# Lines of 65 words instead of 64 for two sources of weights, and an image loaded in chunks

## The chip, the cores and the metric

The kernel runs on one core of one Trainium2 chip. Times are device microseconds (us) of one execution. Before the change the median of three runs was 7750.35 us (7748.62 to 7756.67). Experiments ran in three jobs, each with its own runs of the kernel before on the same chip.

TensorE is called PE where it multiplies and PEld where it loads weights; DVE is VectorE, ACT ScalarE, POOL GpSimd, SP SyncE.

## The reference, cut to what matters

Eight images of 128 x 128 tokens with 64 channels pass two layers in fp32. The first is an attention along columns and rows, which the change does not touch. The second is this:

```python
h = _pw(_ln(x, g1, b1), w_te, b_te)                      # norm over channels, 64 -> 128
F = jnp.fft.fft2(h.astype(jnp.complex64), axes=(1, 2))
fr = jnp.concatenate([jnp.real(F), jnp.imag(F)], axis=-1)
fc = gelu(_pw(fr, w_fc, b_fc))                           # a 256 x 256 map per frequency
sp = jnp.real(jnp.fft.ifft2(re + 1j * im, axes=(1, 2)))  # re, im: the halves of fc
x1 = x + _pw(sp, w_tp, b_tp)
h2 = _pw(_ln(x1, g2, b2), w_fe, b_fe)                    # the MLP: norm, 64 -> 128,
d = gelu(depthwise_conv_3x3(h2, w_dw) + b_dw)            # depthwise convolution,
return x1 + _pw(d, w_fp, b_fp)                           # 128 -> 64
```

## The kernel before

The transforms are products with cosine and sine tables. In both places of interest the data is the *stationary* operand: a channel of the normed image "xn", or of the spectrum "gt", is loaded into TensorE as weights, and the table streams past it. With the channel as the innermost axis, the 128 words of one channel lie 64 words apart.

```python
def load_norm(b):
    xn = xnp.tile([P, P, C], F32, tag="xn", name="xn")       # P = 128, C = 64, one buffer
    nc.sync.dma_start(out=xn, in_=x2[b])                     # 4 MB in one load
    images[b] = {"xn": xn}
    for h in range(0, P, CH):                                # CH = 8: 16 chunks
        norm(xn[:, h : h + CH, :], xn[:, h : h + CH, :], CH)
        yield
```

`norm(xo, xi, n)` reduces on DVE, subtracts the mean on POOL, squares on ACT, reduces again on DVE, and multiplies on POOL. The forward transform along h, in two halves of the frequencies, each followed by its frequency groups:

```python
gt = big.tile([P, 2, 64, C], F32, tag="gt", name="gt")
...
for c0 in range(0, C, 4):
    aps = ps_m.tile([P, 4, P], F32, tag="mm", name="aps")
    for c in range(4):
        nc.tensor.matmul(                                    # line 490
            aps[:, c, 0:nk], lhsT=xn[:, :, c0 + c], rhs=rw[:, first : first + nk],
            start=True, stop=True,
        )
    # evicted to "at" by DVE and ACT in turn
...
nc.scalar.copy(gt[:, :, k0 : k0 + n, :].rearrange("p t k c -> p k t c"), gps[:, 0:n, :, :])
```

The inverse transform:

```python
gr, gi = gt[:, 0, :, c0 + c], gt[:, 1, :, c0 + c]
both = gt.rearrange("p t k c -> p (t k) c")[:, :, c0 + c]
nc.tensor.matmul(yps[:, c, :], lhsT=both, rhs=cosn, start=True, stop=False)          # line 592
nc.tensor.matmul(yps[0:64, c, :], lhsT=gi, rhs=nsinn, start=False, stop=True)        # line 593
nc.tensor.matmul(yps[64:128, c, :], lhsT=gr, rhs=sinn, start=False, stop=True)       # line 594
```

The images follow one another. The MLP of one image and the norm of the image after it are admitted step by step beside the transforms:

```python
NORM_FROM = 20                       # the second step of the second half's groups
...
for i, _ in enumerate(fourier(b)):
    if i * (P // CH + 1) >= done * MLP_STEPS:
        next(before, None)           # the MLP of image b - 1
        done += 1
    if i >= NORM_FROM:
        next(after, None)            # the norm of image b + 1
```

A scheduler then orders the instructions of each engine, so an instruction may run well ahead of its place in this text if its data allow it.

Of the kernel before, what the change touches and what calls it, by code (L numbers as in the profile page):

```python
"""Criss-cross attention followed by a Fourier token mixer and a depthwise-convolution MLP.

Layer 0 attends, per token (h, w), over its image column (its own position excluded) and its row
with one softmax.  Both directions run through the same block routine with the attended axis on the
partitions; each keeps its own row maximum, and the two partial softmaxes are merged afterwards.

Layer 1 runs per image.  The channel maps of the spectral branch commute with the spatial
transforms, so w_te is applied behind the forward FFT (merged with w_fc) and w_tp in front of the
inverse one.  The input is real, so only the frequencies kw = 0..64 are transformed; the map at the
mirrored frequency -k sees the conjugate, i.e. the imaginary weights with the other sign, and the  # L10
real part of the inverse FFT needs only the Hermitian part (G(k) + conj G(-k)) / 2.
"""
# [10 lines left out]
F32 = mybir.dt.float32  # L23
# [4 lines left out]
PSUM = bass.MemoryType.PSUM  # L28
DRAM = bass.MemoryType.DRAM

P = 128
C = 64
D8 = 8
HID = 128
R = 32  # rows (or columns) of an attention block
NBLK = P // R
NEG = -1.0e30
EPS = 1e-3
# Frequencies along w, in the order they are stored in: 0 and 64 share a slot later.
KWS = [0, 64] + list(range(1, 64))  # L40
NKW = len(KWS)
CH = 8  # image rows of a chunk of the convolution
# Of the steps of one image's transforms: those that the MLP is spread over, and the first one behind
# the last use of the normed image.
MLP_STEPS = 28
# [3 lines left out]
def dft_tables():  # L49
    """cos/sin tables of the 128-point transforms; they depend on the shapes alone."""  # L50
    n = np.arange(P)
    kw = np.array(KWS)
    ang = 2.0 * np.pi * (np.outer(n, kw) % P) / P
    rw = np.stack([np.cos(ang), -np.sin(ang), -np.cos(ang)], axis=2).reshape(P, 3 * NKW)
    full = 2.0 * np.pi * (np.outer(n, n) % P) / P
    cos, sin = np.cos(full), np.sin(full)
    k = np.arange(64)
    back = 2.0 * np.pi * (np.outer(k, n) % P) / P
    re = 2.0 * np.cos(back) / P
    re[0] = 1.0 / P  # L60
    im = -2.0 * np.sin(back) / P
    im[0] = np.where(n % 2 == 0, 1.0, -1.0) / P
    idw = np.concatenate([re, im], axis=0)
    out = np.concatenate([rw, cos, sin, cos / P, sin / P, -sin / P, idw], axis=1)
    return np.ascontiguousarray(out.astype(np.float32))
# [5 lines left out]
def attention(tc, nc, x, w_q, b_q, w_k, b_k, w_v, b_v, gamma, x2):  # L71
    NB = x.shape[0]
    with ExitStack() as ctx:
        const = ctx.enter_context(tc.tile_pool(name="a_const", bufs=1))
        xpool = ctx.enter_context(tc.tile_pool(name="a_x", bufs=8))
        big = ctx.enter_context(tc.tile_pool(name="a_big", bufs=1))
        p2 = ctx.enter_context(tc.tile_pool(name="a_p2", bufs=2))
# [10 lines left out]

        # Rows 0-63 of a transposed pair hold the channels of one image line, rows 64-127 those of
        # the next one; the weights are block diagonal accordingly.  # L90
        wq = const.tile([P, 64], F32, tag="wq", name="wq")
# [10 lines left out]
        nc.gpsimd.memset(bq, 0.0)  # L102
        # Row 8 of every quadrant of the keys is a row of ones, which takes up the maximum.
        nc.gpsimd.memset(bk, 1.0)
# [27 lines left out]

        # Line r = 2 * (8 * (q // 2) + i) + q % 2 of a block lies in quadrant q at place i.
        def stage1(xb, mneg):
            """Queries, keys, values and the (negated) maxima of one block; yields between parts."""
            s = Block()
# [4 lines left out]
            for ic in range(2):  # L141
                for g in range(2):
                    jc = 2 * g + ic
                    tp = ps_m.tile([P, 4, P], F32, tag="mm", name="tp")
                    for jj in range(4):
                        r = 2 * (4 * jc + jj)
# [34 lines left out]
            for q in range(4):  # L181
                e = ps_e.tile([P, 8, P], F32, tag="e", name="e1")
                rows = slice(32 * q, 32 * q + D8)
# [16 lines left out]
            for q in range(4):  # L200
                nc.scalar.dma_start(
                    out=s.qt[32 * q + D8 : 32 * q + D8 + 1, :, :],
                    in_=mts[16 * (q // 2) + q % 2 : 16 * (q // 2) + 16 : 2, :],
# [3 lines left out]
        def stage2(s, y, masked):  # L207
            """Attention of one block, not yet divided by its sum (last column); yields between parts."""
            yv = y.rearrange("p (g i s) c -> p g s i c", g=2, s=2)
# [11 lines left out]
            for q in range(4):  # L221
                e = ps_e.tile([P, 8, P], F32, tag="e", name="e2")
                rows = slice(32 * q, 32 * q + D8 + 1)
                for a in range(2):
# [8 lines left out]
                    for j in range(4):  # L233
                        i = 4 * a + j
# [42 lines left out]
        def end(n):  # L277
            b, way, blk = tasks[n]
            s = state.pop(n)
# [16 lines left out]
            o.xs.append(s.xb)  # L296
            # Both partial sums are brought to the common maximum and divided by the common sum.
            cols = slice(blk * R, blk * R + R)
            mh, mw, dh, dw = o.mht[:, cols], s.mneg, o.dht[:, cols], y[:, :, C]
            t = p2.tile([P, 5, R], F32, tag="tsm", name="tsm")  # L300
# [37 lines left out]
        for n in range(len(tasks)):  # L338
            fetch(n + 3)
            parts = [end(n)]  # L340
# [6 lines left out]
def mixer(tc, nc, x2, tbl, prm, out):  # L347
# [3 lines left out]
    with ExitStack() as ctx:  # L351
# [29 lines left out]
        with tc.tile_pool(name="m_prep", bufs=1) as prep:  # L381
# [32 lines left out]

            # Biases of both norms go through the linear maps behind them.
            pv = ps_m.tile([P, 2], F32, tag="mm", name="pv")
# [8 lines left out]

            # w_te @ w_fc for the real and the imaginary half.
            nc.vector.tensor_scalar_mul(wte, wte, col[:, 0:1])
# [18 lines left out]
        def norm(xo, xi, n):  # L446
            """(xi - mean) / sqrt(var + eps) over the channels of n lines of tokens."""
            st = p2.tile([P, 3, CH], F32, tag="st", name="st", bufs=4)
            nc.vector.tensor_reduce(st[:, 0, 0:n], xi, AX.X, ALU.add)
            nc.vector.tensor_scalar_mul(st[:, 0, 0:n], st[:, 0, 0:n], 1.0 / C)  # L450
            nc.gpsimd.tensor_tensor(  # L451
                xo, xi, st[:, 0, 0:n].unsqueeze(2).to_broadcast([P, n, C]), ALU.subtract
            )
            sq = p2.tile([P, CH, C], F32, tag="sq", name="sq")
            nc.scalar.activation(sq[:, 0:n, :], xo, AF.Square)
            nc.vector.tensor_reduce(st[:, 1, 0:n], sq[:, 0:n, :], AX.X, ALU.add)
            nc.vector.tensor_scalar(st[:, 1, 0:n], st[:, 1, 0:n], 1.0 / C, EPS, ALU.mult, ALU.add)  # L457
            nc.gpsimd.tensor_tensor(st[:, 2, 0:n], st[:, 1, 0:n], mhalf[:, 0:n], ALU.pow)  # L458
            nc.gpsimd.tensor_tensor(  # L459
                xo, xo, st[:, 2, 0:n].unsqueeze(2).to_broadcast([P, n, C]), ALU.mult  # L460
            )
# [3 lines left out]
        def load_norm(b):  # L465
            xn = xnp.tile([P, P, C], F32, tag="xn", name="xn")
            nc.sync.dma_start(out=xn, in_=x2[b])
            images[b] = {"xn": xn}
            for h in range(0, P, CH):
                norm(xn[:, h : h + CH, :], xn[:, h : h + CH, :], CH)  # L470
                yield

        # Groups of frequencies that fill a PSUM bank, in two halves that share the buffer "at".
        groups = [KWS[0:2]] + [KWS[k : k + 4] for k in range(2, NKW, 4)]
        halves = [groups[:9], groups[9:]]

        def fourier(b):
            im = images[b]
            xn = im["xn"]
            gt = big.tile([P, 2, 64, C], F32, tag="gt", name="gt")  # L480
            for half_groups in halves:
# [20 lines left out]
                for g in half_groups + [None, None]:  # L502
# [45 lines left out]
                    if pend_tp is not None:  # L548
                        gg, (gr, gi) = pend_tp
                        gps = ps_m.tile([P, 4, 2, C], F32, tag="mm", name="gps")  # L550
                        if gg[0] == 0:
                            # kw = 0 and 64 have real inverse columns: they share one complex slot.
                            nc.tensor.matmul(gps[:, 0, 0, :], lhsT=gr[:, 0, 0:P], rhs=wtp, start=True, stop=False)
# [5 lines left out]
                        else:  # L559
# [7 lines left out]
                        nc.scalar.copy(  # L567
                            gt[:, :, k0 : k0 + n, :].rearrange("p t k c -> p k t c"), gps[:, 0:n, :, :]
                        )
# [39 lines left out]
        def lines(xs, lo, hi):  # L609
            """The rows lo..hi of an image held in two halves, as (offset, rows) pieces."""  # L610
            for s in range(2):
                a, z = max(lo, 64 * s), min(hi, 64 * s + 64)
                if a < z:
                    yield a - lo, xs[s][:, a - 64 * s : z - 64 * s, :]

        def mlp(b):
            """Chunks of image rows; the first half of a chunk goes ahead of the second half of the one before."""
            xs = images.pop(b)["x1"]

            def expand(k, prev):  # L620
# [9 lines left out]
                nc.scalar.copy(xt, tp)  # L630
                # Rows 8k-2 .. 8k+8 of the expanded image with a border of zeros.
                h2 = p2.tile([P, CH + 3, P + 2], F32, tag="h2", name="h2")
# [58 lines left out]

        # The MLP of an image runs beside the first part of the next image's transforms, and the norm
        # of the image after that beside the last part, when "xn" is free again.
        for _ in load_norm(0):
# [58 lines left out]
```

## Time and profile before

| | |
|---|---|
| median of three runs | 7750.35 us |
| attention, all images | until about 3850 us |
| first L490 (image 0) | 3941.3 us |
| one image of the mixer (its first L490 to that of the next image), mean of images 1 to 6 | 464.2 us |
| of it: first half of L490 (F1) / its groups | 54.5 / 138.3 us |
| second half of L490 (F2) / its groups | 54.1 / 129.7 us |
| inverse | 86.0 us |

The stage times come from the order of time: F1 and F2 last from the first to the end of the last L490 of a half, their groups from there to the next stage's first product, and the inverse from the first L592 to the end of the last L594. Some 1.75 us more pass before the next image's first L490. The prediction below shows the page's busy line, the windows of image 4 and the rows of the weight loads. A row of a line's loads gives shortest, median and longest duration in ns, then the first start and the last end in us. One more such row is needed later, that of the 64-column loads of the inverse:

```profile
L593 PEld LDWEIGHTS yps<-tb,gt x1024: 215/234/258, 4159.1 to 7463.3; 128*64 128x64 f32 x171
```

L490 is written 128 times an image, 1024 times in all, and counts x2048, two such records each.

### The profile page before, as it was taken

Reading aid. Unit: us, or ns where it says so; the run is one execution under the profiler, and the core shown is the slowest. Engines: PE = TensorE matmul, PEld = TensorE weight load, DVE = VectorE, ACT = ScalarE, POOL = GpSimd, SP = SyncE. Lnnn points to the kernel's source line nnn. Section 1 sums busy time; section 2 is a strip of 40 time slices with the busy share of each in tenths; the row PEclk is TensorE's granted clock in tenths of the full one; section 3 lists DMA queues with packets and bytes.
Section 4 is the critical chain, followed back from the end, with each engine's and each line's share of the span. In section 5 each row is a group of like instructions: output and inputs, shape, how many; then the busy total and the mean of one; then the engine's idle time right before and its main releaser. Section 6 shows DMA issues by size and latency. Waiting matters only on the chain. (4 is left out here: it accounts for less than half of the span.)

```text
span 7744.1 us, 73804 instructions
## 1 busy us (share of the span) xinstructions
PE 6559.2 (85%) x31019; PEld 5279.1 (68%) x31019; DVE 3369.5 (44%) x4376; ACT 1790.8 (23%) x2458; POOL 2176.4 (28%) x2050
## 2 busy tenths in 40 slices
PE   9999999999999999999668778787877878778774
PEld 7777878778787787777556566565665666566553
DVE  2232322323222232322222665756667565675757
ACT  1111111111111111111022433424333242433422
POOL 0020110201002020020244463544545345463423
PEclk6565555665556555555578778787887878778775
DMA  2010020100202001010100010100101010010000
GB/s 66 2 55 12 6 61 1 55 12 6 60 1 61 6 18 49 1 44 1 46 33 14 22 44 7 44 17 24 41 9 45 17 45 17 22 44 7 24 19 17
DMA packets 188189, 208.21 MB, mean 27 GB/s; under 512 B 141138, under 2 KB 176466, under 8 KB 176594
## 3 DMA queue, kind: packets, MB, share of 16 engines
q1 hardware_dynamic: 179154, 168.89, 7.6%
q0 software_dynamic: 4608, 33.56, 1.2%
q8 instruction: 244, 4.00, 0.2%
q10 hardware_dynamic: 4096, 1.06, 0.1%
q14 instruction: 87, 0.71, 0.0%
HBM read 135.32 MB, written 67.11 MB: 26 GB/s over the span
## 5 line engine op out<-in xcount | busy, mean ns | idle before, releaser
L666 DVE SCALAR_TENSOR_TENSOR acc<-h,wdw,acc 128x1024 f32<-128x1024 f32 (+2 forms) x1088 | 1502.5, 1404 | 33.6 <-ACT acc L664 23.1
L235 PEld LDWEIGHTS e<-qt,kt 9*128 9x128 f32 x4096 | 855.9, 315 | 248.3 <-issue 212.3
L235 PE MATMUL e<-qt,kt 9*128 9x128 f32 x4096 | 958.9, 422 | 70.0 <-DMA qt<-mts 45.5
L314 POOL TENSOR_TENSOR xb<-xb,yw 128x2048 f32<-128x2048 f32 x32 | 132.7, 4148 | 3009.5 <-issue 1918.9
L672 PE MATMUL op<-wfp,acc 128*128 128x64 f32 x2048 | 391.7, 371 | 672.8 <-ACT acc L669 672.8
L672 PEld LDWEIGHTS op<-wfp,acc 128*128 128x128 f32 x2048 | 378.9, 282 | 779.3 <-ACT acc L669 753.4
L218 PEld LDWEIGHTS yp<-v,att 128*128 128x128 f32 x4096 | 810.8, 303 | 132.0 <-ACT qt L177 90.5
L218 PE MATMUL yp<-v,att 128*128 128x65 f32 x4096 | 856.5, 393 | 0.0
L243 ACT ACTIVATE att<-e 128x1024 f32<-128x1024 f32 x256 | 261.9, 1023 | 1825.7 <-PE e L235 1825.7
L185 PEld LDWEIGHTS e<-kt,qt 8*128 8x128 f32 x4096 | 607.6, 256 | 69.9 <-issue 47.8
L185 PE MATMUL e<-kt,qt 8*128 8x128 f32 x4096 | 633.8, 353 | 14.9 <-DVE mh L188 14.9
L458 POOL TENSOR_TENSOR st<-st,mhalf 128x8 f32<-128x8 f32 x256 | 511.6, 1999 | 192.1 <-DVE st L457 128.4
L542 POOL TENSOR_TENSOR gl<-gl 128x512 f32<-128x512 f32 (+2 forms) x272 | 433.2, 1597 | 381.1 <-ACT gl L539 381.1
L490 PE MATMUL aps<-tb,xn 128*128 128x93 f32 (+1 forms) x2048 | 455.3, 405 | 80.1 <-POOL xn L459 80.1
L219 DVE COPY yh<-yp 128x260 f32<-128x260 f32 x256 | 109.6, 428 | 946.8 <-PE yp L218 946.8
L490 PEld LDWEIGHTS aps<-tb,xn 128*128 128x128 f32 x2048 | 453.3, 312 | 90.8 <-POOL xn L459 80.9
L676 POOL TENSOR_TENSOR ot<-x,bfp 128x512 f32<-128x512 f32 (+1 forms) x144 | 216.9, 1511 | 871.8 <-DVE x L607 609.3
L157 PE MATMUL vps<-wv,xt 128*128 128x130 f32 x2048 | 415.8, 373 | 43.3 <-DVE xt L151 43.3
L219 DVE COPY yw<-yp 128x260 f32<-128x260 f32 x256 | 109.6, 428 | 777.3 <-PE yp L218 777.3
L157 PEld LDWEIGHTS vps<-wv,xt 128*128 128x128 f32 x2048 | 372.9, 275 | 75.3 <-DVE xt L151 67.7
L607 DVE TENSOR_TENSOR x<-dps,x 128x256 f32<-128x256 f32 x256 | 167.5, 708 | 515.2 <-PE dps L601 515.2
L327 POOL TENSOR_TENSOR xb<-xb,tm 128x128 f32<-128x128 f32 x512 | 270.0, 580 | 409.9 <-DVE tm L322 409.9
(146 smaller groups left out, 9748.8 us busy)
## 6 DMA issues: line engine op xcount, KB each, us to landing
xb<-in_x_dram SPq DMA_DIRECT2D x32, 1024.0 KB
x<-xb POOLq DMA_DIRECT2D x32, 1024.0 KB, 7.3
x<-x SPq DMA_DIRECT2D x16, 2048.0 KB
xn<-x SPq DMA_DIRECT2D x8, 4096.0 KB
out_dram<-ot SPq DMA_DIRECT2D x120, 256.0 KB
qt<-mts ACTq DMA_DIRECT2D x256, 4.0 KB
out_dram<-ot SPq DMA_DIRECT2D x8, 224.0 KB
xb<-in_x_dram SPq DMA_DIRECT2D x32, 0.2 KB
```

The costliest lines, as they stand in the source:

```text
L157: nc.tensor.matmul(vps[:, jj // 2, o : o + 130], lhsT=xt[:, jj, :], rhs=wv2, start=True, stop=True)
L185: nc.tensor.matmul(e[:, i, :], lhsT=s.qt[rows, i, :], rhs=s.kt[rows, i, :], start=True, stop=True)
L218: nc.tensor.matmul(yp[:, j, :], lhsT=att[:, i, :], rhs=s.v[:, r, :], start=True, stop=True)
L219: nc.vector.tensor_copy(yv[:, q // 2, q % 2, 4 * a : 4 * a + 4, :], yp)
L235: nc.tensor.matmul(e[:, i, :], lhsT=s.kt[rows, i, :], rhs=s.qt[rows, i, :], start=not masked, stop=j == 3 or not masked,)
L243: nc.scalar.activation(att, e, AF.Exp)
L327: nc.gpsimd.tensor_tensor(xv, xv, tm[:, :, k * R : k * R + R], ALU.add)
L458: nc.gpsimd.tensor_tensor(st[:, 2, 0:n], st[:, 1, 0:n], mhalf[:, 0:n], ALU.pow)
L490: nc.tensor.matmul(aps[:, c, 0:nk], lhsT=xn[:, :, c0 + c], rhs=rw[:, first : first + nk], start=True, stop=True,)
L542: nc.gpsimd.tensor_tensor(gl[:, 0, 0:n], gl[:, 0, 0:n], gl[:, 1, 0:n], ALU.add if half == 0 else ALU.subtract,)
L666: nc.vector.scalar_tensor_tensor(out=av, in0=src, scalar=wdw[:, t : t + 1], in1=av, op0=ALU.mult, op1=ALU.add)
L672: nc.tensor.matmul(op[:, i, :], lhsT=acc[:, i, :], rhs=wfp, start=True, stop=True)
```

## The change

The intent is to let the weights be read at a stride that is no multiple of a large power of two, in the hope of cheaper loads. Since one long load into padded lines would fall into short pieces, the image comes in chunks through a small buffer "xi", from which the norm writes into the padded lines. The core of the diff (the rest strips comments, so lines behind it move by two: L490 becomes L492, L592 becomes L594):

```diff
         def load_norm(b):
-            xn = xnp.tile([P, P, C], F32, tag="xn", name="xn")
-            nc.sync.dma_start(out=xn, in_=x2[b])
+            xn = xnp.tile([P, P, C + 1], F32, tag="xn", name="xn")
             images[b] = {"xn": xn}
             for h in range(0, P, CH):
-                norm(xn[:, h : h + CH, :], xn[:, h : h + CH, :], CH)
+                xi = p2.tile([P, CH, C], F32, tag="xi", name="xi")
+                nc.sync.dma_start(out=xi, in_=x2[b][:, h : h + CH, :])
+                norm(xn[:, h : h + CH, 0:C], xi, CH)
                 yield
...
-            gt = big.tile([P, 2, 64, C], F32, tag="gt", name="gt")
+            gt = big.tile([P, 2, 64, C + 1], F32, tag="gt", name="gt")
...
-                            gt[:, :, k0 : k0 + n, :].rearrange("p t k c -> p k t c"), gps[:, 0:n, :, :]
+                            gt[:, :, k0 : k0 + n, 0:C].rearrange("p t k c -> p k t c"), gps[:, 0:n, :, :]
```

The pool of "xi" holds two buffers.

## The prediction

> **What bounds the kernel now.** I read the page's busy line first, then the table of windows cut at the stages of one image, then the rows of single lines and the order of time around the reads that the change touches. The page:
>
> ```profile
> PE 6559.2 (85%) x31019; PEld 5279.1 (68%) x31019; DVE 3369.5 (44%) x4376; ACT 1790.8 (23%) x2458; POOL 2176.4 (28%) x2050
> ```
>
> That average hides two halves. Until about 3850 us the attention runs, which the change leaves alone. Then eight images go through the mixer, one every 464 us, and the last image's MLP runs alone from 7464 us. The windows of image 4 are, in order, the first half of the forward transform along h (L490), its frequency groups, the second half of L490, its groups, and the inverse transform:
>
> ```profile
> core 0: us, PE busy (x) PEld busy (x) DVE busy (x) ACT busy (x) POOL busy (x), PEclk, DMA share, GB/s
> 5638.70:5693.20 54.50, 38.45 (x159) 34.07 (x157) 34.89 (x51) 15.72 (x22) 21.03 (x17) 0.78 0.02 5
> 5693.20:5831.50 138.30, 103.34 (x522) 76.14 (x523) 96.18 (x87) 64.04 (x86) 72.35 (x60) 0.83 0.09 27
> 5831.50:5885.50 54.00, 43.81 (x178) 38.15 (x177) 30.59 (x32) 15.84 (x21) 13.59 (x13) 0.59 0.07 15
> 5885.50:6015.30 129.80, 97.96 (x452) 75.33 (x451) 101.27 (x121) 57.92 (x80) 97.90 (x78) 0.79 0.18 61
> 6015.30:6101.20 85.90, 85.90 (x413) 62.07 (x413) 24.17 (x41) 11.22 (x19) 17.66 (x15) 0.91 0.00 1
> ```
>
> In the inverse TensorE is busy for every microsecond and nothing else comes near: it is the bound. In the two group stages no engine is full; the MLP of the image before hands work round between DVE, ACT, POOL and PE. The two L490 stages lie between: 28 us each are L490, the rest is the MLP's chain.
>
> What the change touches is the reading of weights. L490 takes a channel of "xn" as stationary operand, L592 to L594 a channel of "gt": 128 (or 64) words that lie 64 words apart. The rows of these lines, with two others beside them, L320 (weights from "yh", whose lines have 65 words already) and L508 (contiguous weights); the three numbers are shortest, median and longest in ns:
>
> ```profile
> L490 PEld LDWEIGHTS aps<-tb,xn x2048: 291/312/338, 3941.3 to 7274.8; 128*128 128x128 f32 x187
> L320 PEld LDWEIGHTS tpy<-ident,yh x512: 200/226/336, 469.3 to 3827.5; 128*128 128x128 f32 x171
> L508 PEld LDWEIGHTS fps<-tb,at x1040: 186/192/338, 3970.4 to 7364.1; 128*128 128x128 f32 x174
> L592 PEld LDWEIGHTS yps<-tb,gt x1024: 291/295/337, 4158.5 to 7462.8; 128*128 128x128 f32 x171
> ```
>
> The shortest load is 291 ns at 64 words, 200 at 65, 186 contiguous. Loads overlap, so the rate matters more. These rows (start, length, count) give it:
>
> ```profile
> 5656.76 14.10 PE L490 MATMUL aps<-tb,xn 128*128 128x102 f32 x64
> 7283.11 1.89 PE L672 MATMUL op<-wfp,acc 128*128 128x64 f32 x16
> 954.54 0.57 PEld L320 LDWEIGHTS tpy<-ident,yh 128*128 128x128 f32 x4 [0.81 <-ACT qt L177]
> ```
>
> L490: (14.10 - 0.4)/63 = 217 ns each. L672, contiguous, warm: about 112 ns each. L320 at 65 words, warm: (0.57 - 0.205)/3 = 122 ns. So a stride of 64 words costs a factor of nearly two and 65 almost none, where the clock is full. And only there: two windows of L490 alone,
>
> ```profile
> 5663.00:5667.00 4.00, 4.00 (x20) 4.00 (x19) 1.00 0.01 4
> 4048.00:4052.00 4.00, 4.00 (x20) 4.00 (x20) 0.50 0.00 0
> ```
>
> hold 20 instructions in 4 us at clock 1.00 and at 0.50 alike. Contiguous loads at clock 0.50 start every 213 ns (L672, L218), so a cold clock hides the stride.
>
> **What the Trainium skill says.** "SBUF — State Buffer", section "Door 1: The DMA port swizzle", says that successive reads that each fall in another 16-byte line pay a penalty, and that four fp32 words is as far as one can stride free. By that a stride of 65 words would be as bad as 64, and the trace disagrees: 122 against 217 ns. "TensorE: Matmul & The Clock Gate", Part 1, says that the clock is either half or full and follows TensorE's activity; this trace agrees, its clock records hold only 0.5 and 1.0. The same page, Part 2 step 1, says that loads are pulled ahead under running matmuls; L490 agrees (312 ns long, one each 217 ns), the inverse only in part, as its 128- and 64-column loads alternate (below). No page gives a cost for a stride beyond the line rule.
>
> **The change part by part.** (1) *L490, 65 words.* Per image 256 instructions, 217 to 122 ns warm (saves 95), 218 to 213 cold (saves 5). Image 0 has no MLP beside it: its first half is 28.3 us at clock 0.82, of which some 32 instructions are cold; 96 x 0.095 + 32 x 0.005 = 9 to 10 us. Its second half (29.8 us) starts warm and falls cold after 9 us; 102 moving columns held the clock better than 93, and when the loads no longer starve the array it should hold: I take 12 us. For the other images the MLP chain lies beside it. In the first half, 32 instructions go first, and then TensorE waits 5.6 us for POOL (L459) anyway: 1.3 us saved. Then 64 run while DVE works off an acc chain that L672 waits 8.8 us for; but that DVE chain itself stands behind evictions that wait for L490:
>
> ```profile
> 5665.62 0.85 DVE L498 COPY at<-aps 128x408 f32<-128x408 f32 x1 [2.67 <-PE aps L490]
> 5669.14 0.85 DVE L498 COPY at<-aps 128x408 f32<-128x408 f32 x1 [1.70 <-PE aps L490]
> ```
>
> so some 4 to 5 us come off there, and 1 to 3 from the last 32. I take 7 us in the first half; in the second (clock 0.59, mostly cold, but the 512-column L643 warms it before the run of 64) 6.5 us. The evictions keep up: two engines of 0.85 us for eight instructions of 122 ns.
>
> (2) *The inverse, 65 words.* One channel as the loads show it:
>
> ```profile
> 7028.43 0.51 PEld L592 LDWEIGHTS yps<-tb,gt 128*128 128x128 f32 x2
> 7029.05 0.22 PEld L593 LDWEIGHTS yps<-tb,gt 128*64 128x64 f32 x1
> ...
> 7029.16 0.25 PEld L593 LDWEIGHTS yps<-tb,gt 128*64 128x64 f32 x1
> ...
> 7029.55 0.30 PEld L601 LDWEIGHTS dps<-ys,tb 128*128 128x128 f32 x2
> ```
>
> 0.62 us for the full pair, 0.50 for the halves: 1.12 us, 64 times, plus 16 x 0.86 for L601 makes 85.5 of the 85.9 us. At 65 words the full pair's loads take 122 + 215 = 337 ns instead of 510 (saves 0.17) and the halves in proportion 0.25 instead of 0.37 (saves 0.11): 0.28 us a channel. The stage opens with about 14 us of cold clock, some 11 channels, which save nothing: 53 x 0.28 = 15 us an image. All of it is on the path, since the next image's MLP needs the end of this stage.
>
> (3) *The chunked load.* Image 0's normed copy is waited for in full:
>
> ```profile
> 3941.28 28.24 PE L490 MATMUL aps<-tb,xn 128*128 128x102 f32 x128 [80.10 <-POOL xn L459]
> ```
>
> Of these 80 us, the 4 MB load holds DVE's first reduction until 3879.7; POOL then needs 16 x 3.7 us. In the new order the first two chunks are loaded ahead of the weights and only DVE's preparation, done by about 3864, holds them: 16 us saved, less any time in which a chunk queues behind the 2 MB load of x1. In the other images the load cost little, and 128 loads of 256 KB replace 8 of 4 MB; two buffers and SP's order couple loads and stores, which I count as zero.
>
> Instruction counts on every engine stay the same but SP's 120 more issues; TensorE's order is almost the same. Sum: 16 + (10 + 12 + 15) + 7 x (7 + 6.5 + 15) = 252 us; 7750 - 252 is about 7500 us.
>
> **The rivals.** (a) *Line rule:* 65 words as slow as 64; only the 16 us at the start remain, 7735. L320's 200 ns against 291 speaks against it. (b) *The clock stays or turns cold:* with less work TensorE may be gated more, cold L490 saves nothing and a longer cold start eats the inverse: 12 us an image in the inverse and 5 in L490, about 7600. For it: the clock of 0.59 in the second half. (c) *Small buffer as a new wait:* DVE, in order, waits for a chunk of 2 to 3 us at each step, POOL's norm comes late in the second group stage, where DVE and POOL are at 101 and 98 of 130 us: back 5 to 10 us an image, 7550 to 7580. Against it: SP runs two chunks ahead. (d) *More than I count:* the clock warm through both L490 stages and the norm starting earlier, some 40 us an image, about 7410.
>
> **Range and chances.** Parts (2) and (3) with image 0 alone come to about 160 us, just over 2%; so the 2% line (7595) is passed unless (a), (b) or (c) bites hard. Predicted 7500 us, 8 in 10 within 7410 to 7600. Faster by over 2%: 0.87, within: 0.12, slower: 0.01.
>
> **What would show it.** L490's loads near 200 to 215 ns and warm starts near 122 ns apart; L592's loads the same; the inverse at about 71 us, still full of TensorE; the L490 stages 47 us each, with fewer DVE waits on L490; the first L490 near 3925 us. Wrong would be: loads still at 291, a lower clock in these stages, or group stages that grow by waits on "xi" as much as the others shrink.

## The result, and the profile after

The changed kernel takes 7803.81 us (median of four, 7800.76 to 7806.63) against 7749.84 us (median of four, 7748.62 to 7756.67). The ratio is 1.0068, with a 95% interval of 1.0054 to 1.0083: 0.7% slower, which counts as the same at the 2% mark. A ratio here and below is the mean time of one kernel's runs over that of the other's of the same rounds, so not quite the ratio of the medians quoted. The predicted 7500 us, and the whole range up to 7600, were missed by a wide margin.

The page's busy line of the changed kernel:

```profile
PE 6566.3 (84%) x31019; PEld 5266.0 (67%) x31019; DVE 3368.8 (43%) x4376; ACT 1783.5 (23%) x2458; POOL 2194.4 (28%) x2050
```

Every count is as before, and TensorE is busy for 7 us *more* (6566.3 against 6559.2), where the prediction counted on far less. The windows of image 4 after the change, with the same columns and the same five stages as in the prediction (F1, groups, F2, groups, inverse):

```profile
5663.00:5720.60 57.60, 42.16 (x159) 36.40 (x157) 35.30 (x51) 15.99 (x22) 20.11 (x17) 0.63 0.02 4
5720.60:5859.70 139.10, 100.95 (x524) 74.93 (x523) 97.80 (x91) 63.56 (x86) 73.72 (x60) 0.83 0.09 27
5859.70:5914.30 54.60, 44.42 (x177) 38.81 (x177) 31.67 (x34) 15.88 (x21) 12.27 (x12) 0.56 0.07 15
5914.30:6051.20 136.90, 97.67 (x451) 72.32 (x450) 102.16 (x127) 59.24 (x84) 118.69 (x92) 0.79 0.19 57
6051.20:6135.80 84.60, 84.56 (x413) 60.41 (x414) 18.80 (x28) 8.79 (x15) 1.16 (x2) 0.91 0.01 3
```

The inverse, which was to fall to 71 us, takes 84.6. F1 is longer, with a granted clock of 0.63 where it was 0.78. The second group stage is 7 us longer, and POOL works 118.7 us in it where it worked 97.9; POOL's work has left the inverse in exchange (1.2 us where it was 17.7).

The rows of the weight loads after the change:

```profile
L492 PEld LDWEIGHTS aps<-tb,xn x2048: 303/327/337, 3935.9 to 7337.1; 128*128 128x128 f32 x187
L594 PEld LDWEIGHTS yps<-tb,gt x1024: 302/306/338, 4153.5 to 7524.7; 128*128 128x128 f32 x171
L595 PEld LDWEIGHTS yps<-tb,gt x1024: 190/208/230, 4154.2 to 7525.3; 128*64 128x64 f32 x171
```

The loads of 128 columns have become *longer*, by about 12 ns in the shortest (303 against 291), while the prediction wanted 200 to 215. Only the 64-column loads of the inverse are shorter, 208 instead of 234 ns. In order of time, the L492 of the first half of image 4:

```profile
5663.04 7.48 PE L492 MATMUL aps<-tb,xn 128*128 128x102 f32 x32
5681.31 14.87 PE L492 MATMUL aps<-tb,xn 128*128 128x102 f32 x64
5713.01 7.67 PE L492 MATMUL aps<-tb,xn 128*128 128x102 f32 x32
```

The run of 64 took 14.10 us before. (14.87 - 0.4)/63 is 230 ns each, where it was 217 and where the prediction wrote 122.

At the start, the first L492 comes 5.4 us earlier than the first L490 did (3935.9 against 3941.3), not 16:

```profile
3870.03 2.04 POOL L451 TENSOR_TENSOR xn<-xi,st 128x512 f32<-128x512 f32 x2 [12.88 <-DVE wfe L408]
...
3935.92 1.94 PE L492 MATMUL aps<-tb,xn 128*128 128x102 f32 x7 [69.01 <-POOL xn L459]
```

POOL's first subtraction waits for DVE's preparation (L408), which ends near 3870 us. Part of this is not the change's: the attention, the same program in both, ended 4.3 us later in this profile. Its last work on POOL, before and after:

```profile
3835.42 2.55 POOL L327 TENSOR_TENSOR xb<-xb,tm 128x128 f32<-128x128 f32 x5
3839.70 2.56 POOL L327 TENSOR_TENSOR xb<-xb,tm 128x128 f32<-128x128 f32 x5
```

Counted from the end of these, the first product comes 9.7 us sooner. In the profiles of the thirteen full kernels this end lies between 3838 and 3850 us, so a difference of a few us between two runs' starts tells little.

Stage means over images 1 to 6 (us), with two of the experiments below that add the parts one by one:

| | F1 | groups | F2 | groups | inverse | sum |
|---|---|---|---|---|---|---|
| before | 54.5 | 138.3 | 54.1 | 129.7 | 86.0 | 464.2 |
| chunks alone | 54.5 | 136.8 | 52.9 | 136.2 | 85.9 | 468.0 |
| chunks, xn 65 | 56.9 | 139.3 | 54.7 | 137.0 | 86.2 | 475.8 |
| after (and gt 65) | 57.3 | 139.0 | 54.6 | 137.0 | 84.5 | 474.2 |

(The sum is that of a whole image up to the next image's first L490, so 1.7 us more than the five stages; the means are good to 0.1 us.) So each image is 10.0 us longer: 3.8 from the chunks, 7.8 from the lines of xn, 1.6 back from the lines of gt. Six such images make 60 us of the 60.8 by which the two profiled runs differ (7804.9 against 7744.1); the gain at the start and what images 0 and 7 add nearly cancel. Of the 7.8 us for the lines of xn, 4.3 stand in the two L490 stages; 2.5 stand in the first group stage, which reads no xn, and were not followed further.

### The profile page after: what moved, and what is told of

Read it like the earlier page. It is cut to its first block, busy times and chain, and to the rows that moved or that the text cites. A ratio compares the mean times of both kernels' runs of the same rounds, so it can differ in the third digit from the quotient of the medians. Undisturbed runs are those within 1.5% of the kernel's fastest.

```text
span 7804.9 us, 74100 instructions
## 1 busy us (share of the span) xinstructions
PE 6566.3 (84%) x31019; PEld 5266.0 (67%) x31019; DVE 3368.8 (43%) x4376; ACT 1783.5 (23%) x2458; POOL 2194.4 (28%) x2050
## 4 chain that ended last, share of the span: by engine, by line
PE 66%; DVE 14%; POOL 13%; issue 4%; ACT 3%; DMA 1%; SPq 0%; POOLq 0%; DVEq 0%; ACTq 0%
PE e L235 12%; PE yp L218 11%; DVE acc L668 9%; PE e L185 8%; PE aps L492 5%; PE vps L157 5%; PE pq L170 4%; PE yps L594 4%; POOL st L458 4%; PE yps L595 3%; PE op L674 3%; POOL xb L327 2%; POOL gl L544 2%; PE dps L603 2%; PE hp L645 2%
## 5 line engine op out<-in xcount | busy, mean ns | idle before, releaser
L674 PE MATMUL op<-wfp,acc 128*128 128x64 f32 x2048 | 363.7, 352 | 695.7 <-ACT acc L671 695.7
L674 PEld LDWEIGHTS op<-wfp,acc 128*128 128x128 f32 x2048 | 352.5, 264 | 799.1 <-ACT acc L671 771.0
L492 PE MATMUL aps<-tb,xn 128*128 128x93 f32 (+1 forms) x2048 | 482.0, 427 | 69.0 <-POOL xn L459 69.0
L492 PEld LDWEIGHTS aps<-tb,xn 128*128 128x128 f32 x2048 | 478.2, 327 | 78.6 <-POOL xn L459 69.8
```

The costliest lines, as they stand in the source:

```text
L492: nc.tensor.matmul(aps[:, c, 0:nk], lhsT=xn[:, :, c0 + c], rhs=rw[:, first : first + nk], start=True, stop=True,)
L674: nc.tensor.matmul(op[:, i, :], lhsT=acc[:, i, :], rhs=wfp, start=True, stop=True)
```

## The experiments

**Theory**, formed from the rows above: an ordinary fp32 weight load pays for each word that lies in a line of its own, whatever the stride, so 65 words are no better than 64 and even a little worse; L320, from which the prediction took its 122 ns, is a transpose and a different kind of instruction. **Rival 1**: 65 words are cheap, but a colder clock, or the way the loads alternate, hides it in these stages. **Rival 2**: the lines help, and the chunked load eats the gain.

### The reads by themselves

This kernel computes nothing; its output is zero. It runs 32 fp32 products back to back for each of 16 strides of the stationary operand, behind a warm-up; then the same for transposes, for strided *moving* operands, and for pairs of 64-column weights as in the inverse.

```python
def line(step, n=P, first=0):
    return s[:, first : first + (n - 1) * step + 1 : step]
...
nc.tensor.matmul(ps, lhsT=line(step), rhs=mov[:, 0:64], start=True, stop=True)  # L66, 32 times
nc.tensor.transpose(ps, line(step), ident)                                       # L72
nc.tensor.matmul(ps, lhsT=ident, rhs=line(step), start=True, stop=True)          # L78
nc.tensor.matmul(ps[64 * h : 64 * h + 64, :], lhsT=line(step, 64, 64 * step * h),
                 rhs=mov[:, 0:64], start=True, stop=True)                        # L85
```

> Only TensorE's reads, output zero on purpose: 32 equal products (64 instructions) after a warm-up of 512-column products, for stationary operands of 128 words with steps from 1 to 128 words, for transposes, for strided moving operands and for pairs of 64-word halves. Theory A (the skill's line rule: a step of more than four words costs, whatever it is): steps of 8 words and more all take 210 to 235 ns an instruction at full clock, 64 and 65 alike within 10%, and only 1 (perhaps 2 and 4) takes 110. Theory B (banks: it is the power of two that costs): 63, 65, 66 and 127 take about 110 to 130 ns, and 16, 32, 64 and 128 take 218 or more. My reading of the changed kernel's trace (231 ns at 65) is for A. For why I was misled: if transposes at a step of 64 also take about 125 ns, the transpose itself, not its 65 words, made L320 fast; if they take 218, its lines of 65 words did.

The one run took 631.12 us, by itself. From the view in order of time, the weight loads of some strides (start, length of the whole row, count):

```profile
26.89 7.11 PEld L66 LDWEIGHTS w_one<-mov,src 128*128 128x128 f32 x63 [0.24 <-issue]
44.34 7.50 PEld L66 LDWEIGHTS w_two<-mov,src 128*128 128x128 f32 x63 [0.23 <-issue]
61.74 15.21 PEld L66 LDWEIGHTS w_four<-mov,src 128*128 128x128 f32 x64 [0.24 <-issue]
...
194.81 14.22 PEld L66 LDWEIGHTS w_sixtyfour<-mov,src 128*128 128x128 f32 x64 [0.24 <-issue]
221.42 15.02 PEld L66 LDWEIGHTS w_sixtyfive<-mov,src 128*128 128x128 f32 x64 [0.24 <-issue]
```

And of the transposes (which leave one record each, where a product leaves two):

```profile
436.88 3.42 PEld L72 LDWEIGHTS transpose_one<-ident,src 128*128 128x128 f32 x31 [0.29 <-issue]
450.68 4.62 PEld L72 LDWEIGHTS transpose_sixtyfour<-ident,src 128*128 128x128 f32 x31 [0.21 <-issue]
465.64 3.91 PEld L72 LDWEIGHTS transpose_sixtyfive<-ident,src 128*128 128x128 f32 x31 [0.23 <-issue]
```

A row's length less one load's own duration, over the count less one, gives the distance of starts: for one word (7.11 - 0.19)/62 = 112 ns. The medians of the distances, from start to start, to within 1 ns:

| stride in words | 1 | 2 | 4 | 8 | 16 | 32 | 63 | 64 | 65 | 66 | 68 | 72 | 80 | 96 | 127 | 128 |
|---|---|---|---|---|---|---|---|---|---|---|---|---|---|---|---|---|
| ns | 112 | 118 | 233 | 238 | 219 | 217 | 230 | 218 | 230 | 243 | 233 | 238 | 218 | 217 | 230 | 218 |

| stride in words | 1 | 64 | 65 | 128 |
|---|---|---|---|---|
| transposes, ns each | 109 | 147 | 123 | 147 |
| strided moving operand, ns | 112 | 220 | 230 | 220 |
| two loads of 64 columns, mean ns a pair | 58 | 146 | 117 | not run |

This settles the disputed cost. From two words to four the cost doubles and then stays: four words apart is where each word has one of the page's 16-byte lines (which the prediction names) to itself. Among the wide strides, the multiples of 16 words are the *cheapest*, 217 to 219 ns, and 65 words take 230: precisely what L492 shows in the changed kernel. A transpose pays far less, and there 65 words do save 24 of 147 ns, and 122 ns is what L320 showed. The pairs of halves gain from 65 too.

The clock does not hide a gain. Windows over the loads at 64 and at 65 words, cut in thirds (columns: length, PE, PEld, DVE, POOL, then the granted clock):

```profile
194.80:199.80 5.00, 5.00 (x24) 4.85 (x23) 0.00 (x0) 0.00 (x0) 1.00 0.00 0
199.80:204.40 4.60, 4.60 (x23) 4.60 (x23) 0.00 (x0) 0.00 (x0) 0.56 0.00 0
204.40:209.00 4.60, 4.60 (x23) 4.60 (x23) 0.00 (x0) 0.00 (x0) 0.50 0.00 0
221.40:226.40 5.00, 5.00 (x23) 4.85 (x21) 0.00 (x0) 0.00 (x0) 1.00 0.00 0
```

About 23 loads pass in each third whether the clock is full or half, and 65 words at the full clock are no faster. Rival 1 falls. The windows show a second thing: PE and PEld are busy without a gap, and the clock falls to half all the same. It did so 4.9 to 6.3 us into each of the fourteen runs at strides of four words and more. With contiguous weights it stayed at 1.00, over a run of 7.5 us, and also over the 14 us in which the *moving* operand was strided, where the products followed one another just as slowly (220 ns).

### The chunks alone

```diff
+                xi = p2.tile([P, CH, C], F32, tag="xi", name="xi")
+                nc.sync.dma_start(out=xi, in_=x2[b][:, h : h + CH, :])
+                norm(xn[:, h : h + CH, :], xi, CH)          # xn and gt keep 64 words
```

> The chunked load through the small buffer alone, lines stay 64 words. If the small buffer and the order that comes with it cost the time (my theory): 7775 to 7795 us, 25 to 45 us over before, the second group stage of an image at 136 to 138 us instead of 129.7, with POOL busy about 119 us in it instead of 98, and a start about 5 us earlier. If the lines of 65 words cost all of it: 7740 to 7755 us and group stages as before.

7762.40 us (7758.73 to 7772.34), against 7750.98 for the kernel before (nine runs): ratio 1.0015 [1.0002, 1.0029]. The loss is smaller than expected: the start gives 5 us back, and the groups behind F1 give 1.5 us an image and F2 1.2. The cost lies in the second group stage alone, here of image 4:

```profile
5885.30:6021.50 136.20, 99.77 (x452) 74.30 (x451) 102.36 (x127) 59.44 (x84) 118.49 (x92) 0.76 0.20 57
```

Rival 2 has a grain of truth, 11 us, but not the size. Where the time comes from is followed up below.

### The lines of the spectrum alone

```diff
-            gt = big.tile([P, 2, 64, C], F32, tag="gt", name="gt")
+            gt = big.tile([P, 2, 64, C + 1], F32, tag="gt", name="gt")
```

> Only the spectrum has lines of 65 words. My theory: single 128-word loads 306 instead of 295 ns, but the two 64-word halves that load at once 191 instead of 219, so the inverse stage is 84.5 instead of 86.0 us and the run about 7738 us (minus 8 to 14). If 65 words are bad for all reads: 7755 to 7775.

7744.81 us (7732.70 to 7755.24), ratio 0.9988 [0.9976, 1.0001]. The inverse of image 4:

```profile
6016.00:6100.30 84.30, 84.30 (x413) 60.36 (x414) 24.57 (x41) 11.21 (x19) 17.68 (x15) 0.91 0.00 1
```

It is 1.6 us shorter than the 85.9 before, full of TensorE as ever: the full loads lost 12 ns each, the halves gained more. The gain of 15 us an image does not exist. Nor does the program clearly gain (the interval holds 1): the first group stage is 2.0 us longer here, so that an image takes 464.2 us as before.

### The lines of the image alone

```diff
-            xn = xnp.tile([P, P, C], F32, tag="xn", name="xn")
-            nc.sync.dma_start(out=xn, in_=x2[b])
+            xn = xnp.tile([P, P, C + 1], F32, tag="xn", name="xn")
+            nc.sync.dma_start(out=xn[:, :, 0:C], in_=x2[b])
```

> Only the normed image has lines of 65 words, loaded whole straight into them (so in 256-byte pieces). My theory: L490 every 231 instead of 218 ns, the first stage of an image 57.3 instead of 54.5 us and the second 54.6 instead of 54.1: about 25 us more, plus whatever the slower load of pieces costs at the start (up to 20 us): 7770 to 7800 us. If 65 words cost nothing: 7750 to 7770, all of it in the start.

7869.81 us (7869.15 to 7872.28), ratio 1.0151 [1.0137, 1.0165]: worse than expected. F1 goes to 57.8 us at a clock of 0.63, but the second group stage also grows to 139.3 us, and the first L490 comes at 3951.5 us, 10 us later than before. The load now falls into pieces of 64 words, so this run changes two things, and the share of the padding cannot be read from it. A cleaner one was needed.

### The lines of the image, on top of the chunks

```diff
-            xn = xnp.tile([P, P, C], F32, tag="xn", name="xn")
+            xn = xnp.tile([P, P, 65], F32, tag="xn", name="xn")     # beside "xi"; gt keeps 64
```

> The changed kernel but with 64-word lines in the spectrum: the chunk and the normed image's 65 words. By the stages of the runs so far the 65 words of the normed image cost about 50 us and those of the spectrum give back about 10: 7800 to 7825 us, first stage 57.3 us at a clock of 0.63, second 54.6, inverse 85.9. If the parts do not add up so, below 7790.

7820.64 us (7817.80 to 7825.12), ratio 1.0091 [1.0077, 1.0106]. F1 of image 4, to be set against 54.50 us at a clock of 0.78 before:

```profile
5665.80:5721.90 56.10, 40.27 (x159) 35.77 (x157) 35.18 (x51) 15.71 (x22) 20.96 (x17) 0.65 0.02 5
```

So the lines of xn cost the most, some 58 us on top of the chunks (7820.6 - 7762.4, across two jobs), and the lines of gt give some 17 back (7803.8 against 7820.6). That these differences add up to the whole (11 + 58 - 17 is 52, and the change costs 54) follows from how they are formed and proves nothing; the lines of gt by themselves gave only 6 (7744.8 against 7751.0). The stages of the table above are the better measure.

### A padded line whose reads are cheap

Is it the rate of the reads, or the padding itself? Lines of 80 words are padded more, but 80 is a multiple of 16.

```diff
-            xn = xnp.tile([P, P, C], F32, tag="xn", name="xn")
+            xn = xnp.tile([P, P, 80], F32, tag="xn", name="xn")     # beside "xi"; gt keeps 64
```

> The chunked load with lines of 80 words in the normed image, the spectrum at 64. In e1 a step of 80 words loads in 218 ns like 64, and 65 in 230. If the slower read is what 65 words cost in the L490 stages (theory): as the chunk alone, 7755 to 7775 us, first stage 54 to 55 us at a clock of 0.78. If it is the padded lines as such (POOL's, DVE's or ACT's accesses): 7795 to 7815 like the changed kernel, first stage 57 us at 0.63.

7759.05 us (7756.46 to 7762.34), ratio 1.0012 [1.0000, 1.0025], the same as the chunks alone. F1 of image 4:

```profile
5643.60:5698.00 54.40, 38.31 (x159) 33.93 (x157) 34.87 (x51) 15.73 (x22) 21.00 (x17) 0.78 0.02 5
```

54.4 us and a clock of 0.78, as before the change. So padding as such costs nothing; what the lines of 65 words cost goes with the 12 ns by which they are slower to read, and the lower clock goes with it too. The other engines' work on xn does not tell the two apart: with lines of 64, 65 and 80 words the median subtraction and multiplication on POOL take 1042 ns and the square on ACT 630.

### The spectrum by channel

If contiguous weights give what the prediction hoped to get from 65 words, the chain of its argument behind the rate was sound. Here the frequencies of one channel lie side by side.

```diff
-            gt = big.tile([P, 2, 64, C], F32, tag="gt", name="gt")
+            gt = big.tile([P, C, 2, 64], F32, tag="gt", name="gt")
-                            gt[:, :, k0 : k0 + n, :].rearrange("p t k c -> p k t c"), gps[:, 0:n, :, :]
+                            gt[:, :, :, k0 : k0 + n].rearrange("p c t k -> p k t c"), gps[:, 0:n, :, :]
-                gr, gi = gt[:, 0, :, c0 + c], gt[:, 1, :, c0 + c]
-                both = gt.rearrange("p t k c -> p (t k) c")[:, :, c0 + c]
+                gr, gi = gt[:, c0 + c, 0, :], gt[:, c0 + c, 1, :]
+                both = gt[:, c0 + c, :, :].rearrange("p t k -> p (t k)")
```

> Nothing of the change: the spectrum of before stored channel by channel, so that the weights of the inverse are contiguous, while ACT writes it with a step of 128 words. Theory (only contiguous weights read at full speed, e1: 112 ns against 218): an inverse stage of 64 to 69 us instead of 86.0, still full of TensorE, ACT's copy into the spectrum about 1100 ns instead of 585, run 7590 to 7650 us. If the bound of the inverse is something else than these reads, the stage stays above 80 us and the run above 7700.

7622.62 us (7619.41 to 7631.09) against 7749.74: ratio 0.9837 [0.9824, 0.9851]. The inverse of image 4, and the row of its full loads:

```profile
5962.60:6031.40 68.80, 68.80 (x413) 40.44 (x414) 24.02 (x41) 11.41 (x20) 17.33 (x15) 0.90 0.00 1
```

```profile
L592 PEld LDWEIGHTS yps<-tb,gt x1024: 185/189/339, 4170.2 to 7348.1; 128*128 128x128 f32 x171
```

The stage falls from 86 to 69 us, still full of TensorE. ACT writes the spectrum scattered instead of in lines, a copy takes 1052 ns instead of 585, as expected, and no stage pays for it: the stages other than the inverse add up to within 1.5 us of before.

### Both by channel

The image as well: the norm works in "xi", and its last multiplication writes the channel's line.

```diff
-            xn = xnp.tile([P, P, C], F32, tag="xn", name="xn")
-            nc.sync.dma_start(out=xn, in_=x2[b])
+            xn = xnp.tile([P, C, P], F32, tag="xn", name="xn")
...
+                xi = p2.tile([P, CH, C], F32, tag="xi", name="xi")
+                nc.sync.dma_start(out=xi, in_=x2[b][:, h : h + CH, :])
+                norm(xi, xi, CH, xn[:, :, h : h + CH].rearrange("p c h -> p h c"))
...
-                            aps[:, c, 0:nk], lhsT=xn[:, :, c0 + c], rhs=rw[:, first : first + nk],
+                            aps[:, c, 0:nk], lhsT=xn[:, c0 + c, :], rhs=rw[:, first : first + nk],
```

> Normed image and spectrum both stored channel by channel, the image loaded in chunks through a small buffer that is normed in place, its last multiply writing with a step of 128 words. Theory: L490 about 112 ns apart when warm, first and second stage of an image some 47 us each, the inverse 64 to 69 us; POOL's multiply may cost more than 1.04 us for its strided write. That is the gain that I predicted for 65 words: run 7480 to 7580 us. If the L490 stages are set by the MLP's chain, they stay above 52 us and the run is within 20 us of e5.

7496.93 us (7490.66 to 7507.26), ratio 0.9671 [0.9658, 0.9684]. F1 and the inverse of image 4:

```profile
5505.70:5551.10 45.40, 26.45 (x159) 22.17 (x157) 34.43 (x51) 15.95 (x23) 21.00 (x17) 0.77 0.02 5
...
5871.90:5941.10 69.20, 69.19 (x413) 40.69 (x414) 22.75 (x40) 10.53 (x19) 11.07 (x9) 0.89 0.06 16
```

With loads at the contiguous rate F1 takes 45.4 us (predicted for the changed kernel: 47), the inverse 69 (predicted: 71), and the program 7497 (predicted: 7500). This is the prediction's number, reached by another layout, and the close agreement is in part luck. An image is 28.1 us shorter where 28.5 were predicted, but the two L490 stages gave 17.7 us (predicted 13.5) and the inverse 17.0 (15), while the second group stage took 6.4 back (0). Image 0 gave 54 us (37), and the start gave nothing: the first L490 came at 3948.6 us, 7 later than before, where 16 earlier were predicted.

### Why the chunks lengthen the second group stage

The waits of that stage name POOL's subtraction: with the chunks it writes into xn, so it must wait until the last L490 has read xn, and POOL, which works in order, stands still. The chunks-alone kernel, image 4:

```profile
POOL xn L451 <- PE aps L491: 11.7, 1, 11.7
```

(The three numbers are the total in us, the times and the longest.) The first idea was that this wait of 11.7 us is the loss. If the subtraction stays in "xi" and only the last multiplication writes xn, the wait comes later or goes:

```diff
-                norm(xn[:, h : h + CH, :], xi, CH)
+                norm(xi, xi, CH, xn[:, h : h + CH, :])      # the last multiply alone writes xn
```

> The chunked load with 64 words, but the subtraction writes back into the small buffer and only the last multiply writes the normed image, so no early POOL instruction waits for the old image to be free. If that wait at the head of POOL's queue (12 us at the start of each second group stage) costs the 6.5 us that the chunk adds there (theory): second group stage 128 to 132 us, run 7710 to 7740. If it is the load latency or the norm's crowding into that stage: still 135 to 138 us, run 7750 to 7780.

7766.91 us (7761.57 to 7774.15), ratio 1.0023 [1.0010, 1.0035]. No gain:

```profile
5892.80:6028.60 135.80, 94.00 (x451) 70.11 (x450) 94.33 (x111) 56.45 (x79) 101.50 (x80) 0.79 0.18 51
```

The wait fell to 6.1 us (it is now the multiplication's), POOL's work in the stage fell from 118.5 to 101.5 us, and the stage takes what it took. So this theory fell, and with it another: that the loss is simply more POOL work in the stage.

The next idea was the place of the norm. Before, its first reduction cannot start until the whole 4 MB of the next image have arrived, for which xn must be free. A chunk in "xi" needs nothing of the kind, and the scheduler moves it forward. The first two reductions of the next image's norm, on DVE, beside image 4; before the change, where the stage begins at 5885.5 us:

```profile
5906.72 0.68 DVE L449 TENSOR_REDUCE st<-xn 128x8 f32<-128x512 f32 x1
5909.00 0.67 DVE L449 TENSOR_REDUCE st<-xn 128x8 f32<-128x512 f32 x1
```

With the chunks alone, where the stage begins at 5885.3 us:

```profile
5808.98 0.69 DVE L449 TENSOR_REDUCE st<-xi 128x8 f32<-128x512 f32 x1 [2.88 <-POOL xc L459]
5828.92 0.67 DVE L449 TENSOR_REDUCE st<-xi 128x8 f32<-128x512 f32 x1
```

21 us *behind* the beginning of the stage became 76 us *ahead* of it. So the norm was admitted nine steps later, at the first step of the inverse:

```diff
-NORM_FROM = 20
+NORM_FROM = 29                                              # otherwise the chunks alone
```

> The chunked load with 64 words and the norm of the next image admitted nine steps later (from step 29 on, not 20). In the built program DVE and POOL then take the norm's pieces between the MLP's at about the places of the kernel before: after 83, 88, 98, 104 of an image's acc operations, where before has 94, 95, 99, 100 and the plain chunk 56, 68, 88, 88. If the earlier place of the norm is what the chunk costs in the second group stage (theory): 127 to 131 us there and 7715 to 7745 us in all. If it is the small buffer and its loads: still 134 to 138 us and 7750 to 7780.

7736.78 us (7734.57 to 7738.38), ratio 0.9983 [0.9969, 0.9997]: 0.17% faster than before, where the chunks alone were 0.15% slower. The first reduction of the norm, for a stage that begins at 5872.9 us, and the stage itself:

```profile
5862.22 0.67 DVE L449 TENSOR_REDUCE st<-xi 128x8 f32<-128x512 f32 x1
```

```profile
5872.90:6000.90 128.00, 94.83 (x451) 70.76 (x450) 93.20 (x105) 56.62 (x79) 101.94 (x77) 0.81 0.18 51
```

128.0 us, shorter even than before, and the wait of POOL for L491 is still there with 11.7 us, so that wait does not set the length of the stage. The busy times of all five engines are within 1.2 us of those of the run that failed just above, and the stage is 7.8 us shorter. In this stage it is the order of the work and not its amount. Much of the gain goes elsewhere: against the chunks alone, the inverse is 2.3 us longer (88.2 us on the mean) and the first group stage 2.1 (138.8). An image takes 464.5 us, where it took 468.0 with the chunks alone and 464.2 before them: the later norm undoes the loss, and what is faster than before is the start and image 0.

The last question was whether the buffer has any part in it. The chunks can be loaded straight into xn:

```diff
-                xi = p2.tile([P, CH, C], F32, tag="xi", name="xi")
-                nc.sync.dma_start(out=xi, in_=x2[b][:, h : h + CH, :])
-                norm(xn[:, h : h + CH, :], xi, CH)
+                nc.sync.dma_start(out=xn[:, h : h + CH, :], in_=x2[b][:, h : h + CH, :])
+                norm(xn[:, h : h + CH, :], xn[:, h : h + CH, :], CH)
```

> The same chunks, but each loaded straight into its lines of the normed image and normed there, so without the small buffer; the norm's pieces come early here too (after 88, 88, 88, 88, 100 acc operations). If the early place costs (theory): second group stage 134 to 139 us, run 7755 to 7785. If it is the small buffer: 128 to 131 us, run 7725 to 7745.

7840.99 us (7839.22 to 7841.79), ratio 1.0117 [1.0103, 1.0131], and the stage of image 4:

```profile
5930.20:6076.70 146.50, 95.24 (x452) 68.91 (x451) 103.55 (x133) 58.66 (x84) 112.80 (x92) 0.77 0.16 51
```

Without the small buffer the loss is larger than was expected, so a loss needs no small buffer. Both ranges were missed. The first reductions stand here 3 and 4 us behind the beginning of the stage, where in the kernel before they are at 21 and 24. Which chain makes 146.5 us of this was not followed further, and that stays open, as does the exact chain by which the earlier norm delays the MLP in the chunks-alone kernel; TensorE's waits for the convolution (L672 for "acc") are 28.0 us before, 25.1 with the chunks and 24.1 with the later norm, which tells nothing.

### The best version

By channel, with the later norm:

```diff
-NORM_FROM = 20
+NORM_FROM = 29                                              # otherwise both by channel
```

> The best so far, both tensors by channel, with the norm admitted from step 29 on. If the early place of the norm costs there too (second group stage 136.0 us in it), that stage falls to 126 to 131 us and the run to 7430 to 7465. If the place does not matter: 7490 to 7505.

7426.27 us (7418.96 to 7434.85) against 7751.16, ratio 0.9582 [0.9569, 0.9594]: 4.2% faster than the kernel before, a little better than expected, and faster than the changed kernel by nearly 5%. The second group stage of image 4:

```profile
5694.40:5819.90 125.50, 90.41 (x452) 67.11 (x451) 84.63 (x93) 58.83 (x76) 85.29 (x67) 0.83 0.16 44
```

In both-by-channel with the early norm this stage took 136.6 us; the inverse stays at 69.0.

## Why the prediction was wrong

**The bound (right).** The inverse is bound by TensorE: 84.6 of 84.6 us busy after the change, 68.8 of 68.8 when the loads are contiguous. Shortening a load there shortens the stage, and the stage shortens the program.

**The rate at 65 words, in parts (1) and (2) (wrong, and this decided it).** The prediction wrote "a stride of 64 words costs a factor of nearly two and 65 almost none", and took 122 ns from L320. But L320 differs from L490 in two things: its stride, and that it is a transpose, which leaves one record where a product leaves two. The view of its row says only LDWEIGHTS and does not show this; the count does (x512 for 64 channels of eight images, against x2048 for L490's 128 products an image). TensorE's transpose is a mode of its own, as the Trainium skill says in "TensorE: Matmul & The Clock Gate", Part 4. In the reads by themselves a transpose took 147 ns at 64 words and 123 at 65, a product 218 and 230. The trace of before held no ordinary product at any stride but 1 and 64, so it could not tell the stride's effect from the transpose's. The prediction weighed the line rule of "SBUF — State Buffer" against this row and overruled the page. The measured 112, 118 and 233 ns at strides of 1, 2 and 4 words agree with the page's rule of two hits on a line; the prediction's reading does not.

**Part (1), L490: -7 and -6.5 us an image predicted, +2.8 and +0.5 measured.** Each read became 12 to 13 ns slower, 256 x 13 ns = 3.3 us an image. In F1 the granted clock fell with it from 0.78 to 0.63. Lines of 80 words, read at 218 ns, kept 54.4 us and 0.78.

**Part (2), the inverse: -15 us predicted, -1.5 measured.** The full loads lost and the halves gained. With contiguous loads the same stage gave 17 us.

**Part (3), the start: -16 us predicted, -5.4 measured.** The path was right and the term mis-sized. DVE's preparation, done by 3864.1 us in the trace of before, ended near 3870, as POOL's wait of 12.88 us for L408 shows; 4.3 us of that are the later end of the attention. From POOL's first subtraction to the first product it then took 65.9 us (3870.0 to 3935.9) and not the 60.1 of before (3881.2 to 3941.3): DVE waited 2.9 us for the third chunk to arrive, and only 0.2 to 0.3 us for each of the others behind it. The loss by the chunks was also put at zero for the other images; it is 3.8 us each.

**Rival (a), the line rule (right in kind, and given too little).** It put the time at 7735; the runs gave 7804, because 65 words are not as slow as 64 but slower, and because of the chunks. **Rival (b), the clock:** it did fall in F1, but as a companion of slower reads, and no cheap read was hidden by it. (Its own sum is off: 17 us an image on top of 7500 is about 7636 and not 7600.) **Rival (c), the small buffer:** its 5 to 10 us an image in the second group stage are near the 6.5 measured with the chunks alone, but not for its reason: in the trace of the chunks alone no engine waits for a load of "xi" beside image 4. Admitting the norm later took the loss away with the same buffer, and loading without the buffer made it larger. **Rival (d):** the 40 us an image were there for loads that are in truth contiguous (464.2 - 423.4 = 40.8 in the best version). That the numbers meet is chance: the norm was admitted later there, not earlier, and the granted clock was still 0.75 in F1 and 0.69 in F2.

**The range.** The chance of 0.12 for "the same" was the chance of being wrong on one rate on which 236 of the 252 us rested. One row of another instruction kind was a thin base for that. What stood behind the rate held: with loads that are in truth cheap, the L490 stages and the inverse shrank by what was predicted or a little more.

## What to carry to other kernels

Before a rate is carried from one row of a profile to another, make sure that the two instructions differ in one thing only: same operation, same number of records for a product, same dtype; otherwise measure the rate by itself first. For fp32 weights, padding a line does not make a strided read cheap; laying the read axis side by side does, and moving the scatter to the engine that writes the tile was nearly free here (1.5 us an image, beside the 17 us of the inverse). And if work is made free to start earlier, look at where the scheduler puts it: here admitting the norm nine steps later was worth 26 us (7762 against 7737, across two jobs), of which 21 stand in images 1 to 6. That is more than the chunks had ever gained at the start.

## What the Trainium skill lacked or had wrong

- "SBUF — State Buffer", section "Door 1: The DMA port swizzle": its rule of two hits per 16-byte line is confirmed for TensorE's fp32 weights (112 and 118 ns at strides of 1 and 2 words, 233 at 4). Its figure of four fp32 words as how far one can stride free is too high: two words are nearly free, four cost the double.
- No page has it that among strides beyond the line, multiples of 16 words are the cheapest: 217 to 219 ns at 16, 32, 64, 80, 96 and 128 words, against 230 at 63, 65 and 127, 238 at 8 and 72, and 243 at 66.
- No page gives the cost of a strided *moving* fp32 operand: 220 ns at 64 words and 230 at 65, against 112 contiguous.
- "TensorE: Matmul & The Clock Gate", Part 4, gives no time for an fp32 transpose (its table of terms has a factor only) nor its dependence on the stride: 109 ns at 1 word, 147 at 64, 123 at 65. A pair of 64-column weight loads has the same order: 58, 146 and 117 ns.
- The same page, Part 1, says that activity releases the throttle, and not how time counts in which TensorE is held up by its weight loads. With full loads at strides of four words and more, the profile shows TensorE busy without a gap, and the clock still fell from 1.00 to 0.50 after 4.9 to 6.3 us. With contiguous weights it stayed at 1.00, also at the same slow pace (220 ns, strided moving operand, 14 us), and so it did with pairs of 64-column loads at 64 words (9.5 us). No run shows why.
